# Shared expert of a macaron layer: two groups at once, its down product in the two row halves of the array

## The chip, the cores and the metric

The kernel runs on one core of one Trainium2 chip. The metric is the device time of one execution in microseconds; the median of several runs is compared. All data is float32. Engines: PE is TensorE (matrix products into PSUM), DVE is VectorE, ACT is ScalarE, POOL is GpSimd, SP issues DMAs.

## The reference, cut to what matters

`x` is 8 sequences of 1024 rows of 128. Each goes through an FFN with half weight, attention, and the same FFN again:

```
x = x + 0.5 * ffn(layernorm(x))
x = x + attention(layernorm(x))        # rotary, causal, one head of 128
x = x + 0.5 * ffn(layernorm(x))

ffn(xt):                               # 16 experts of 64 units, top 4 of them
    scores = sigmoid(xt @ gate_w.T);  idx = top_k(scores + gate_b, 4)
    comb   = 2.5 * scores / sum(scores over idx), at idx, else 0
    y      = sum over e of comb[:, e] * ((silu(xt @ g_e.T) * (xt @ u_e.T)) @ w2_e.T)
    return y + (silu(xt @ g_s.T) * (xt @ u_s.T)) @ w2_s.T     # shared expert, 64 units
```

All 16 experts are computed for every row and weighted by `comb`. The last line is the shared expert, the part that the change is about.

## The kernel before, in words

**Groups and periods.** A group is 512 rows (4 tiles of 128) of one sequence in one of the two FFN layers; there are 32. One group is the work of one *period*. The activations are held transposed, `hT` (128 features x 512 rows). Periods 2n and 2n+1 are the two halves of one sequence in one layer.

**A period** has slots U0 to U8 and D0 to D8. Slot U(k+1) follows `up(k)` for k = 0 to 7: two products with `hT`, 128 units of gate into bank 2(k%2)+1 (L276) and of up into bank 2(k%2) (L277), then Silu on ACT (`sg`, L279), gate times up on DVE (`hid`, L281), and times the expert weights `cb` on POOL (`hidT`, L282). Then `down(k)` for k = 0 to 7 accumulates 128 units after 128 units into bank 0, which is `y` (L288).

**The shared expert before.** `up_shared` opens every period: one product with `ws`, whose 128 columns are 64 gate and 64 up units, into bank 5 (L266); Silu of its upper 64 partitions into `ss` (L268); DVE multiplies into rows 64 to 127 of `shared` (L269). Rows 0 to 63 of `shared` and of the weights `wsd` hold zeros. `down(8)` is a full product with them, the ninth that accumulates into `y`; then DVE copies `y` to `yT` (L291). In the next period at U3, `add` turns `yT` back (L296) and adds half of it to `x` (L299).

**Jobs between.** Everything else is put into slots by hand, with `at(period, slot, job)`; `run` issues the jobs of a slot after the product of that slot. The order on each engine is the order in which the program issues; nothing reorders it afterwards. Jobs that matter here:

- normalisation and router of the group that comes next or after next: `norm_a`, `norm_b`, `turn`, `route_a` (four products of 128 rows to 32 columns in the four column tiles of the array, L192), `route_b` (L201), `score` (Exp, L206), `top_a` and `top_b` (DVE, at D8), `top_c` (DVE, at U1 of the next period, ends with `comb`, L238), and `spread` at U3: a turn of `comb` on PE (L247), a copy on ACT (L249), DMAs to DRAM and back as `cb` (L251, L257). For group 1 they all lie in period 0, `score` at D0 to `spread` at D4.
- two or three queries a period (periods 3 to 28), each of 128 rows of attention: `scores` (L368 and DVE L372 to L375), `exp` (L379), `turn` of the probabilities (L395, copies L399 on ACT and L401 on DVE), `attend` (L407), which adds to `x` on DVE (L411) and takes statistics (L144, L145). The first query attends at D7, the second turns at D8 and attends at U2 of the next period. In most odd periods a third takes scores at D4 into banks 4 and 5 and turns at U3 and U4 of the next period.
- `project` of a half sequence to q or k (L335, bank 5 or 4; two ACT copies L339 and L340; DVE L341; POOL L342 and L343), at U3 and U4 of two periods for each sequence.

**Banks.** 0 to 3 rotate for `up`, 0 is `y` as well, 4 and 5 serve the shared expert, projections and scores; 6 and 7 alternate for all small jobs (`other_bank`). Whoever writes a bank waits until its reader is done: the first up product of a period (L277, bank 0) waits for the copy of `y`, and a turn at U3 waits for L411 or an L399 two jobs earlier.

Of the kernel before, what the change touches and what calls it, by code (L numbers as in the profile page):

```python
# [9 lines left out]
F32 = mybir.dt.float32  # L10
AF = mybir.ActivationFunctionType
ALU = mybir.AluOpType
# [3 lines left out]
P = 128  # L16
# [10 lines left out]
def kernel(  # L27
# [14 lines left out]
    nc = tc.nc  # L42
# [3 lines left out]
    I = w_sh_down.shape[0]  # L46
# [3 lines left out]
    W = GT * P  # L50
    EI = E * I
    NP = EI // P
# [3 lines left out]
    const = ctx.enter_context(tc.tile_pool(name="const", bufs=1))  # L56
# [3 lines left out]
    work = ctx.enter_context(tc.tile_pool(name="work", bufs=3))  # L60
    big = ctx.enter_context(tc.tile_pool(name="big", bufs=2))
# [6 lines left out]
    def bank(i, n=1):  # L68
        return psum[:, i * W : (i + n) * W]
# [3 lines left out]
    def other_bank():  # L73
        spare[0] += 1
        return bank(6 + spare[0] % 2)

    def tiles_of(ap):
        return ap.rearrange("p (j q) -> p j q", q=P)
# [34 lines left out]
    ws = const.tile([P, 2 * I], F32, name="ws")  # L113
# [8 lines left out]
    wd = const.tile([P, NP, D], F32, name="wd")  # L122
    nc.sync.dma_start(out=wd, in_=w_down.rearrange("(n p) d -> p n d", p=P))

    wsd = const.tile([P, D], F32, name="wsd")
    nc.gpsimd.memset(wsd[:I, :], 0.0)
    nc.sync.dma_start(out=wsd[I:, :], in_=w_sh_down)
    shared = []
    for n in range(2):
        sh = const.tile([P, W], F32, name=f"shared{n}")  # L130
        nc.gpsimd.memset(sh[:I, :], 0.0)
        shared.append(sh)
    wqkv = const.tile([P, 3, D], F32, name="wqkv")
    cs = const.tile([P, 2, S], F32, name="cs")

# [2 lines left out]
    def stats(key, b, tiles):  # L138

        if key not in mvs:  # L140
            mvs[key] = small.tile([P, NT, 2], F32, tag="mv", name=f"mv_{key}", bufs=16)
        for t in tiles:
            st = small.tile([P, 6], F32, tag="st", name=f"st_{key}_{t}")
            nc.vector.bn_stats(st, xs[b][:, t, :])  # L144
            nc.vector.bn_aggr(mvs[key][:, t, :], st)  # L145
# [26 lines left out]
    class Group:  # L172
        def __init__(self, layer, b, g, n):
            self.layer, self.b, self.g, self.n = layer, b, g, n
            self.nm = f"{layer}_{b}_{g}"
            self.key = f"f{layer}_{b}"
# [82 lines left out]
                        in_=pairs[h, ns, :].unsqueeze(0).broadcast_to([I, NP // 2, W]),  # L259
                    )  # L260

        def up_shared(self):
            self.hidT = big.tile([P, NP, W], F32, tag="hidT", name=f"hidT_{self.nm}")
            self.sh = shared[self.n % 2]
            s_ps = bank(5)
            nc.tensor.matmul(s_ps, ws, self.hT, start=True, stop=True)  # L266
            ss = work.tile([P, W], F32, tag="sg", name=f"ss_{self.nm}")
            nc.scalar.activation(ss[I:, :], s_ps[:I, :], AF.Silu)  # L268
            nc.vector.tensor_tensor(self.sh[I:, :], s_ps[I:, :], ss[I:, :], ALU.mult)  # L269

        def up(self, k):

            nm = f"{self.nm}_{k}"
            units = slice(k * P, (k + 1) * P)
            g_ps, u_ps = bank(2 * (k % 2) + 1), bank(2 * (k % 2))
            nc.tensor.matmul(g_ps, wg[:, units], self.hT, start=True, stop=True)  # L276
            nc.tensor.matmul(u_ps, wu[:, units], self.hT, start=True, stop=True)  # L277
            sg = work.tile([P, W], F32, tag="sg", name=f"sg_{nm}")
            nc.scalar.activation(sg, g_ps, AF.Silu)  # L279
            hid = self.hidT[:, k, :]  # L280
            nc.vector.tensor_tensor(hid, u_ps, sg, ALU.mult)  # L281
            nc.gpsimd.tensor_tensor(hid, hid, self.cb[:, k, :], ALU.mult)  # L282

        def down(self, k):
            if k == 0:
                self.y = bank(0)
            w, h = (wd[:, k, :], self.hidT[:, k, :]) if k < NP else (wsd, self.sh)
            nc.tensor.matmul(self.y, w, h, start=(k == 0), stop=(k == NP))  # L288
            if k == NP:
                self.yT = work.tile([P, W], F32, tag="yT", name=f"yT_{self.nm}", bufs=2)  # L290
                nc.vector.tensor_copy(self.yT, self.y)  # L291

        def add(self):
            yp = tiles_of(other_bank())
            for j in range(GT):
                nc.tensor.transpose(yp[:, j, :], self.yT[:, j * P : (j + 1) * P], ident)  # L296
            tiles = slice(self.g * GT, (self.g + 1) * GT)
            xg = xs[self.b][:, tiles, :]
            nc.vector.scalar_tensor_tensor(xg, yp, 0.5, xg, ALU.mult, ALU.add)  # L299
            if self.layer == 1:  # L300
                nc.sync.dma_start(
                    out=out[self.b].rearrange("(t p) d -> p t d", p=P)[:, tiles, :], in_=xg
                )

# [113 lines left out]
    for b in range(LAG, B):  # L420
        order += [(1, b - LAG), (0, b)]
    order += [(1, b) for b in range(B - LAG, B)]
    groups = [
        Group(layer, b, g, 2 * n + g) for n, (layer, b) in enumerate(order) for g in range(NG)
    ]
# [3 lines left out]
    jobs = {}  # L429

    def at(p, slot, *fs):
        jobs.setdefault((p, slot), []).extend(fs)
# [3 lines left out]
    def when(p, slot):  # L436
        return p * len(slots) + slots.index(slot)
# [28 lines left out]
    for b in range(B):  # L466
        h, st = heads[b], starts[b]
        ready = when(turn_of[0, b, 1] + 1, "U7")
        if b == 0:
            p0, p1 = st - 1, st - 1  # L470
            places = ("U8", "D0", "D2", "D3", "D5", "D6", "D7", "D8")
        else:
            p0, p1 = st - 2, st - 1
            places = ("D0", "D3", "D5", "D8", "U1", "U3", "U4", "U6")
        assert ready < when(p0, places[0])
        at(p0, places[0], h.deviations)
        at(p0, places[1], lambda h=h: h.norm(0))
        at(p0, places[2], lambda h=h: h.norm(1))
        at(p0, places[3], lambda h=h: h.turn(0))
        at(p1, places[4], lambda h=h: h.turn(1))  # L480
        at(p1, places[5], lambda h=h: h.project(0, 0))
        at(p1, places[6], lambda h=h: h.project(1, 0))
        at(p1, places[7], lambda h=h: h.values(0))
        at(st, "U3", lambda h=h: h.project(0, 1))
        at(st, "U4", lambda h=h: h.project(1, 1))
        at(st, "U6", lambda h=h: h.values(1))


    for p, gr in enumerate(groups):
        steps = (  # L490
            gr.norm_a, gr.norm_b, gr.turn, gr.route_a, gr.route_b, gr.score, gr.top_a, gr.top_b,
            gr.top_c, gr.spread,
        )
        if p == 1:
            places = [(0, s) for s in ("U1", "U2", "U5", "U6", "U8", "D0", "D1", "D2", "D3", "D4")]
        else:
            places = [(p - 2, s) for s in ("U5", "D1", "D4", "D5", "D7", "D7", "D8", "D8")]
            places += [(p - 1, "U1"), (p - 1, "U3")]
        if p > 0:
            for f, place in zip(steps, places):  # L500
                at(*place, f)
        if gr.layer == 1:
            for t in range(gr.g * GT, (gr.g + 1) * GT):
                assert done[gr.b, t] < when(p - 2, "U5")

        at(p + 1, "U3", gr.add)
        if gr.layer == 0:
            t = gr.g * GT
            for s in ("U5", "U7"):
                at(p + 1, s, lambda b=gr.b, t=t: stats(f"a{b}", b, (t, t + 1)))  # L510
                t += 2


    for b in range(2, B):
        p = turn_of[0, b, 0]
# [13 lines left out]
    def run(p, slot):  # L529
        for f in jobs.pop((p, slot), []):  # L530
            f()

    gr = groups[0]
# [13 lines left out]
    load_attention()  # L547
    load_x(1, 1)
    for p, gr in enumerate(groups):
        gr.up_shared()  # L550
        run(p, "U0")
        for k in range(NP):
            gr.up(k)
            run(p, f"U{k + 1}")
        for k in range(NP + 1):
            gr.down(k)
            run(p, f"D{k}")
    for p in (NPER, NPER + 1):
        for slot in slots:
# [73 lines left out]
```

## Time and profile before

| | us |
|---|---|
| runs shown: median (lowest to highest of 3) | 1019.27 (1018.79 to 1019.46) |
| profiled execution: own time | 1019.8 |
| profiled execution: span | 1018.0 |
| PE busy | 985.1 (97% of the span) |
| DVE busy | 664.4 (65%) |
| ACT busy | 427.1 (42%) |
| POOL busy | 452.1 (44%) |

The span is from the first to the last instruction on the engines; the execution's own time is 1.8 us longer. The page's mean duration of one instruction is from its start to its modelled end; for PE, where products are pipelined, the distance between the starts of neighbours is shorter than that, and the busy time of a group counts overlaps once. "Idle before" in a row is how long that engine stood idle just ahead of instructions of that row, and "<-" names what ended it.

### The profile page before, as it was taken

The page shows a single profiled execution, that of the slowest core. Times are in us where ns is not written, and L with a number is a line of the kernel's source. Part 1 is how long each engine was busy: PE and PEld are TensorE (multiplying, and loading weights), DVE is VectorE, ACT ScalarE, POOL GpSimd, SP SyncE. Part 2 cuts the span into 40 slices and gives each one's busy share as a digit, 9 for nine tenths or more (in the row PEclk, how much of TensorE's full clock was granted, in tenths as well). Part 3 has the DMA queues.
Part 4 walks back from the last instruction along what each step waited for, and adds up shares of the span by engine and source line. Part 5 has one row for each costly group of instructions (what it writes and reads, how often), then busy time and mean ns, then how long its engine had stood idle before and what let it go on. Part 6 is the DMA issues. An engine that isn't in the chain of part 4 may idle for free.

```text
span 1018.0 us, 11428 instructions
## 1 busy us (share of the span) xinstructions
PE 985.1 (97%) x3552; PEld 511.5 (50%) x3552; DVE 664.4 (65%) x2033; ACT 427.1 (42%) x766; POOL 452.1 (44%) x382
## 2 busy tenths in 40 slices
PE   5799999999999999999999999999999999999998
PEld 2344445554555455545554455555554555455443
DVE  3566877667775767667677665766667756665542
ACT  2243544443544454434444444443444444443321
POOL 1445834365425553345525464334644355323433
PEclk9899999999999999999999999999999999999999
DMA  5384331343214530345213451234412342134440
GB/s 149 99 181 105 84 67 30 72 104 85 46 40 94 116 78 9 82 95 115 59 26 85 95 115 40 45 84 94 95 37 51 82 95 66 43 81 95 95 94 22
DMA packets 56750, 80.23 MB, mean 79 GB/s; under 512 B 3504, under 2 KB 23280, under 8 KB 56560
## 3 DMA queue, kind: packets, MB, share of 16 engines
q1 hardware_dynamic: 55680, 78.36, 34.6%
q10 hardware_dynamic: 1008, 1.13, 0.3%
q8 instruction: 28, 0.46, 0.2%
q14 instruction: 34, 0.28, 0.1%
HBM read 74.24 MB, written 5.24 MB: 78 GB/s over the span
## 4 chain that ended last, share of the span: by engine, by line
PE 85%; DVE 9%; issue 2%; ACT 2%; DMA 1%; POOL 0%; SPq 0%; ACTq 0%; POOLq 0%; DVEq 0%
PE psum L288 24%; PE psum L277 18%; PE psum L276 18%; PE psum L368 6%; PE psum L407 6%; PE psum L395 3%; PE psum L335 3%; PE psum L167 2%; PE psum L266 2%; DVE hidT L281 2%; DVE sel L232 1%; PE psum L349 1%; PE psum L192 1%; PE psum L296 1%; DMA cb<-cd 1%
## 5 line engine op out<-in xcount | busy, mean ns | idle before, releaser
L282 POOL TENSOR_TENSOR hidT<-hidT,cb 128x512 f32<-128x512 f32 x256 | 324.2, 1271 | 536.8 <-DVE hidT L281 489.7
L277 PE MATMUL psum<-hT,wu 128*128 128x512 f32 x512 | 263.2, 596 | 5.1 <-DVE hidT L281 5.1
L276 PE MATMUL psum<-hT,wg 128*128 128x512 f32 x512 | 263.5, 596 | 0.0
L279 ACT ACTIVATE sg<-psum 128x512 f32<-128x512 f32 x256 | 152.7, 597 | 231.8 <-PE psum L276 218.9
L288 PE MATMUL psum<-hidT,wd 128*128 128x512 f32 x512 | 246.5, 599 | 0.0
L281 DVE TENSOR_TENSOR hidT<-psum,sg 128x512 f32<-128x512 f32 x256 | 175.2, 686 | 99.9 <-PE psum L277 97.2
L277 PEld LDWEIGHTS psum<-hT,wu 128*128 128x128 f32 x512 | 97.8, 191 | 129.2 <-issue 103.8
L288 PEld LDWEIGHTS psum<-hidT,wd 128*128 128x128 f32 x512 | 89.9, 190 | 80.7 <-issue 74.4
L276 PEld LDWEIGHTS psum<-hT,wg 128*128 128x128 f32 x512 | 89.2, 192 | 65.4 <-issue 62.8
L407 PEld LDWEIGHTS psum<-v,prT 128*128 128x128 f32 x576 | 74.4, 192 | 30.6 <-issue 26.3
L399 ACT COPY prT<-psum 128x512 f32<-128x512 f32 (+2 forms) x64 | 32.4, 506 | 108.1 <-PE psum L395 107.4
L407 PE MATMUL psum<-v,prT 128*128 128x128 f32 x576 | 74.6, 275 | 0.0
L368 PE MATMUL psum<-k,q 128*128 128x512 f32 (+2 forms) x192 | 72.4, 486 | 0.0
L158 DVE TENSOR_SCALAR xn_f<-x,mv_f,rs_f 128x128 f32<-128x128 f32 x128 | 65.8, 574 | 6.5 <-POOL rs_f L151 6.4
L411 DVE SCALAR_TENSOR_TENSOR x<-psum,rl,x 128x128 f32<-128x128 f32 x64 | 22.1, 346 | 68.3 <-PE psum L407 38.9
L395 PEld LDWEIGHTS psum<-ident,pr 128*128 128x128 f32 x288 | 36.7, 141 | 50.2 <-issue 34.2
L368 PEld LDWEIGHTS psum<-k,q 128*128 128x128 f32 x192 | 36.5, 190 | 45.9 <-issue 45.2
L374 DVE TENSOR_REDUCE top<-psum 128x1 f32<-128x128 f32 (+3 forms) x64 | 48.5, 757 | 2.2
L395 PE MATMUL psum<-ident,pr 128*128 128x128 f32 x288 | 47.4, 274 | 1.9 <-DVE x L299 1.9
L379 ACT ACTIVATE pr<-psum,top 128x128 f32<-128x128 f32 (+3 forms) x64 | 47.7, 746 | 0.3
L372 DVE TENSOR_TENSOR psum<-psum,causal 128x128 f32<-128x128 f32 x64 | 19.0, 297 | 42.4 <-PE psum L368 42.0
L268 ACT ACT_TABLE_LOAD x31 | 39.8, 1283 | 8.9 <-PE psum L266 8.8
(81 smaller groups left out, 988.9 us busy)
## 6 DMA issues: line engine op xcount, KB each, us to landing
cb<-cd SPq DMA_DIRECT2D x128, 512.0 KB, 7.9
x<-in_x SPq DMA_DIRECT2D x16, 256.0 KB, 10.4
out_x<-x SPq DMA_DIRECT2D x16, 256.0 KB, 2.4
cd<-cT SPq DMA_DIRECT2D x32, 32.0 KB, 1.9
cs<-in_rope SPq DMA_DIRECT2D x1, 1024.0 KB, 12.1
wd<-in_w_down SPq DMA_DIRECT2D x1, 512.0 KB, 7.8
wg<-in_w_gate ACTq DMA_DIRECT2D x2, 256.0 KB, 7.2
wu<-in_w_up ACTq DMA_DIRECT2D x2, 256.0 KB, 6.4
```

The source lines that it names most:

```text
L158: nc.vector.tensor_scalar(xn[:, j, :], xs[b][:, t, :], mvs[key][:, t, 0:1], rstd[:, j : j + 1], ALU.subtract, ALU.mult,)
L276: nc.tensor.matmul(g_ps, wg[:, units], self.hT, start=True, stop=True)
L277: nc.tensor.matmul(u_ps, wu[:, units], self.hT, start=True, stop=True)
L279: nc.scalar.activation(sg, g_ps, AF.Silu)
L281: nc.vector.tensor_tensor(hid, u_ps, sg, ALU.mult)
L282: nc.gpsimd.tensor_tensor(hid, hid, self.cb[:, k, :], ALU.mult)
L288: nc.tensor.matmul(self.y, w, h, start=(k == 0), stop=(k == NP))
L368: nc.tensor.matmul(s[:, c:e], h.q[:, i * P : width], h.k[:, c:e], start=True, stop=True)
L374: nc.vector.tensor_reduce(top, s[:, :width], AX.X, ALU.max)
L379: nc.scalar.activation(self.pr[:, : self.width], self.s[:, : self.width], AF.Exp, bias=self.top, scale=SCALE, accum_out=self.h.rl[:, self. ...
L395: nc.tensor.transpose(tp[:, j, :], self.pr[:, (k + j) * P : (k + j + 1) * P], ident)
L407: nc.tensor.matmul(o, self.prT[:, j, :], self.h.v[:, j, :], start=(j == 0), stop=(j == i))
```

## The change

Periods 2n and 2n+1 get one shared expert, the new class `Shared`. Its `up` is two products with `ws`, one for each group, into banks 5 and 4; two Silus; DVE puts the first group's 64 units in rows 0 to 63 of one tile `h`, and the second's in rows 64 to 127. Its `down` is four products of 64 rows by 256 columns: `wsd` now holds the weights twice, in both row halves, and `tile_position=(n * I, 0)` puts group n's product in the upper or lower 64 rows of the array, into bank 5 or 4. ACT copies both results to SBUF (`ys`). `down(k)` ends with k = 7, and `close`, in the place of the ninth product, adds `y` and `ys` into `yT` on DVE.

In even periods `Shared.up` is the first job of U0 and `Shared.down` is at U2; for pair 0 they are at D0 and D3 of period 0, `up` ahead of `score`. `project` moves from U3 and U4 to U4 and U5 (for sequence 0 the first two projections keep their places in period 2).

```diff
     wsd = const.tile([P, D], F32, name="wsd")
-    nc.gpsimd.memset(wsd[:I, :], 0.0)
-    nc.sync.dma_start(out=wsd[I:, :], in_=w_sh_down)
-    shared = []
     for n in range(2):
-        sh = const.tile([P, W], F32, name=f"shared{n}")
-        nc.gpsimd.memset(sh[:I, :], 0.0)
-        shared.append(sh)
+        nc.sync.dma_start(out=wsd[n * I : (n + 1) * I, :], in_=w_sh_down)
...
-        def up_shared(self):
-            self.hidT = big.tile([P, NP, W], F32, tag="hidT", name=f"hidT_{self.nm}")
-            self.sh = shared[self.n % 2]
-            s_ps = bank(5)
-            nc.tensor.matmul(s_ps, ws, self.hT, start=True, stop=True)
-            ss = work.tile([P, W], F32, tag="sg", name=f"ss_{self.nm}")
-            nc.scalar.activation(ss[I:, :], s_ps[:I, :], AF.Silu)
-            nc.vector.tensor_tensor(self.sh[I:, :], s_ps[I:, :], ss[I:, :], ALU.mult)
-
...
         def down(self, k):
             if k == 0:
                 self.y = bank(0)
-            w, h = (wd[:, k, :], self.hidT[:, k, :]) if k < NP else (wsd, self.sh)
-            nc.tensor.matmul(self.y, w, h, start=(k == 0), stop=(k == NP))
-            if k == NP:
-                self.yT = work.tile([P, W], F32, tag="yT", name=f"yT_{self.nm}", bufs=2)
-                nc.vector.tensor_copy(self.yT, self.y)
+            nc.tensor.matmul(
+                self.y, wd[:, k, :], self.hidT[:, k, :], start=(k == 0), stop=(k == NP - 1)
+            )
+
+        def close(self):
+
+            self.yT = work.tile([P, W], F32, tag="yT", name=f"yT_{self.nm}", bufs=2)
+            nc.vector.tensor_tensor(self.yT, self.y, self.ys, ALU.add)
...
+    class Shared:
...
+        def up(self):
+            self.h = work.tile([P, W], F32, tag="sh", name=f"sh_{self.pair[0].nm}", bufs=1)
+            for n, gr in enumerate(self.pair):
+                nc.tensor.matmul(bank(5 - n), ws, gr.hT, start=True, stop=True)
+            for n, gr in enumerate(self.pair):
+                s_ps = bank(5 - n)
+                ss = work.tile([P, W], F32, tag="sg", name=f"ss_{gr.nm}")
+                nc.scalar.activation(ss[I:, :], s_ps[:I, :], AF.Silu)
+                nc.vector.tensor_tensor(
+                    self.h[n * I : (n + 1) * I, :], s_ps[I:, :], ss[I:, :], ALU.mult
+                )
+
+        def down(self):
+            H = W // 2
+            for c in (slice(0, H), slice(H, W)):
+                for n in range(2):
+                    rows = slice(n * I, (n + 1) * I)
+                    nc.tensor.matmul(
+                        bank(5 - n)[:, c], wsd[rows, :], self.h[rows, c], start=True, stop=True,
+                        tile_position=(n * I, 0),
+                    )
+            for n, gr in enumerate(self.pair):
+                gr.ys = work.tile([P, W], F32, tag="ys", name=f"ys_{gr.nm}", bufs=2)
+                nc.scalar.copy(gr.ys, bank(5 - n))
...
-            places = ("D0", "D3", "D5", "D8", "U1", "U3", "U4", "U6")
+            places = ("D0", "D3", "D5", "D8", "U1", "U4", "U5", "U6")
...
-        at(st, "U3", lambda h=h: h.project(0, 1))
-        at(st, "U4", lambda h=h: h.project(1, 1))
+        at(st, "U4", lambda h=h: h.project(0, 1))
+        at(st, "U5", lambda h=h: h.project(1, 1))
...
+        if p % 2 == 0:
+            pair = Shared(groups[p : p + 2])
+            if p == 0:
+                at(0, "D0", pair.up)
+                at(0, "D3", pair.down)
+            else:
+                jobs[p, "U0"] = [pair.up] + jobs.get((p, "U0"), [])
+                at(p, "U2", pair.down)
...
     for p, gr in enumerate(groups):
-        gr.up_shared()
         run(p, "U0")
...
         for k in range(NP + 1):
-            gr.down(k)
+            if k < NP:
+                gr.down(k)
+            else:
+                gr.close()
             run(p, f"D{k}")
```

More of the change, by code (lines that the diff above doesn't have):

```diff
@@ L260, in spread @@
                     )
-        def up_shared(self):
-            self.hidT = big.tile([P, NP, W], F32, tag="hidT", name=f"hidT_{self.nm}")
-            self.sh = shared[self.n % 2]
-            s_ps = bank(5)
-            nc.tensor.matmul(s_ps, ws, self.hT, start=True, stop=True)
-            ss = work.tile([P, W], F32, tag="sg", name=f"ss_{self.nm}")
-            nc.scalar.activation(ss[I:, :], s_ps[:I, :], AF.Silu)
-            nc.vector.tensor_tensor(self.sh[I:, :], s_ps[I:, :], ss[I:, :], ALU.mult)
         def up(self, k):
+            if k == 0:
+                self.hidT = big.tile([P, NP, W], F32, tag="hidT", name=f"hidT_{self.nm}")
             nm = f"{self.nm}_{k}"
@@ L303, in add, with __init__ @@
                 )
+    class Shared:
+        def __init__(self, pair):
+            self.pair = pair
+        def up(self):
[21 more added lines that the diff above has]
+                nc.scalar.copy(gr.ys, bank(5 - n))
     class Heads:
```

## The prediction

> **What bounds the kernel now.** I read the page's busy times and its chain first, then the groups by line, then the timeline of single period ends, where the change acts.
>
> ```profile
> PE 985.1 (97%) x3552; PEld 511.5 (50%) x3552; DVE 664.4 (65%) x2033; ACT 427.1 (42%) x766; POOL 452.1 (44%) x382
> ...
> PE 85%; DVE 9%; issue 2%; ACT 2%; DMA 1%; POOL 0%; SPq 0%; ACTq 0%; POOLq 0%; DVEq 0%
> ```
>
> TensorE is the bound nearly everywhere, and VectorE owns most of the rest of the chain. So PE time taken out is span saved, as long as VectorE does not end later there.
>
> ```profile
> L266 PE MATMUL psum<-hT,ws 128*128 128x512 f32 x64 | 33.6, 608 | 0.0
> L288 PE MATMUL psum<-shared,wsd 128*128 128x512 f32 x64 | 32.8, 593 | 0.0
> L192 PE MATMUL psum<-hT,gw 128*32 128x128 f32 x256 | 13.9, 289 | 0.7 <-ACT hT L168 0.7
> L269 DVE TENSOR_TENSOR shared<-psum,ss 64x512 f32<-64x512 f32 x32 | 22.2, 695 | 9.1 <-ACT ss L268 8.4
> L291 DVE COPY yT<-psum 128x512 f32<-128x512 f32 x32 | 22.1, 691 | 28.9 <-PE psum L288 27.9
> L268 ACT ACT_TABLE_LOAD x31 | 39.8, 1283 | 8.9 <-PE psum L266 8.8
> ```
>
> Each 512-column product leaves two records (64 for 32 calls). In the timeline, starts of such records in a row lie 0.429 us apart: 0.858 us a product, which is the price I use, not the mean duration (records overlap). By the same measure 256 columns take 0.216 us a record (scores, L368).
>
> The end of period 6, and slot U3 of period 7:
>
> ```profile
> 229.97 0.59 PE L288 MATMUL psum<-hidT,wd 128*128 128x512 f32 x1
> 230.40 0.39 PE L407 MATMUL psum<-v,prT 128*128 128x128 f32 x2
> ...
> 230.73 1.02 PE L288 MATMUL psum<-shared,wsd 128*128 128x512 f32 x2
> 230.88 0.35 DVE L411 SCALAR_TENSOR_TENSOR x<-psum,rl,x 128x128 f32<-128x128 f32 x1 [4.66 <-PE psum L407]
> ...
> 231.79 0.69 DVE L291 COPY yT<-psum 128x512 f32<-128x512 f32 x1
> 231.81 1.02 PE L266 MATMUL psum<-hT,ws 128*128 128x512 f32 x2
> ...
> 232.91 1.28 ACT L268 ACT_TABLE_LOAD   x1 [0.53 <-PE psum L266]
> ...
> 233.53 0.59 PE L277 MATMUL psum<-hT,wu 128*128 128x512 f32 x1
> ```
>
> ```profile
> 238.91 0.34 DVE L411 SCALAR_TENSOR_TENSOR x<-psum,rl,x 128x128 f32<-128x128 f32 x1
> ...
> 239.31 0.30 PE L247 MATMUL psum<-ident,comb 128*64 128x128 f32 x1 [0.45 <-DVE x L411]
> ```
>
> Two things to see. The copy of y ends at 232.48, and the first u product, which overwrites y's bank 0, starts at 233.53: 1.05 us to spare. And at U3 PE already waits for VectorE, whose queue holds, between them, top_a, top_b, the shared product, hid 0, top_c, hid 1 and this L411.
>
> **The Trainium skill.** "TensorEngine Tiling (Array Packing)", Tiling Modes: tiles run in parallel, and a change of mode drains the array; Gotcha 1 there asks for different PSUM banks for different row tiles, which the change gives (banks 5 and 4). The trace agrees for column tiles: the next product follows 0.35 us after the four router products below (L192, eight records) began, where eight records of 128 columns in a row take 8 x 0.109 = 0.87; and 0.093 us is lost on entry and on exit (a down product ahead of them takes 0.522 for 0.429, their last record 0.202 for 0.109).
>
> ```profile
> 291.80 0.42 PE L192 MATMUL psum<-hT,gw 128*32 128x128 f32 x8
> 292.15 0.70 PE L288 MATMUL psum<-hidT,wd 128*128 128x512 f32 x1
> ```
>
> "TensorE: Matmul & The Clock Gate", Part 3: four row tiles measured 3.07x. No run here shows row tiles. Its Part 1 says ScalarE and VectorE are strict FIFO; the trace agrees, and this is what makes the waits below.
>
> **The change, part by part.** Period p's last routed down product is "d7". All below is relative to it. A change at a boundary is taken up to U3 of the next period.
>
> 1. Down product: 16 pairs lose 2 x 0.858 = 1.716 us and get four 64-row calls of 256 columns, 8 records. If the two row halves run side by side: 4 x 0.216 + 2 x 0.093 = 1.05 us. If a call's two records keep order ahead of the next tile: 5 x 0.216 + 0.19 = 1.27. If nothing overlaps: 8 x 0.216 + 0.19 = 1.91. I take 1.05, since L192's first records of all four tiles start 7 ns apart.
>
> 2. Up product: same count (32), but two at even periods, none at odd ones. PE between d7 and U3 thus loses 1.716 us into an odd period, and into an even one it gains 1.05.
>
> 3. VectorE: L269 stays at 32 x 0.695, two in even periods, none in odd. L291 becomes an add from PSUM and SBUF; hid (L281) has those operands and takes 0.686, so nothing. ScalarE: 32 ys copies at 0.586 (L168's form) = 18.8 us more. At U2 ys waits for the packed product, with sg 2 behind it: packed start T, ys done T+2.45, sg 2 T+3.05; u 2 ends T+2.97, so hid 2 loses 0.1 at most. ACT has room (42%). Table loads (62 in both programs) don't change; in odd periods sg 0 meets it 0.858 earlier than ss did.
>
> 4. project moves one slot later (U3 to U4, U4 to U5): same work. POOL's two 1.27 us steps behind each move with it; hidT 7 is now ready 3.6 us or more before its down product, which covers it. With L341 out of the way of L299, a 0.54 us wait of L395 at U4 (periods 6, 8, 12, 18, 26) goes; a 0.40 us wait at U3 for ACT's prT copy, hidden by project until now, comes.
>
> 5. One DMA more on SP for wsd (0.5 us at 4 us; SP is then idle until 15.5), three memsets fewer on POOL: nothing.
>
> **What VectorE gives back.** Removing the shared down does not let yT start sooner: L145, which ends the L411 work ahead of it, ends at 231.77 anyway. So into odd periods u 0 comes 1.716 earlier and meets y's bank: period 7 waits 0.7. Then at U3 the chain moves only by the missing L269, 0.70 to 0.74, since top_b ends just when ss did (4.82 and 4.83 after d7). So where PE waits at U3 already, or nearly (into 7, 13, 17, 21, 27), the gain is 0.72 to 0.94, 3.9 together, not 1.716 each. Into 3, where project's L341 is ahead of yT and comb (L238) ends 0.1 before PE needs it, it is nothing. In the other ten L411 ends 0.5 to 1.4 us ahead of PE and VectorE, which waits for ss there, starts hid 0 1.4 to 1.8 sooner, or there is no attention (1, 31) and yT starts 1 us sooner with y: 1.716 less a u 0 wait of 0 to 0.17: about 1.64, 16.4 together. Odd: -20.3.
>
> Into even periods PE pays 1.05, VectorE 0.70 or less. Into 2, 4, 14, 24, 30 a U3 wait of about 0.4 to 0.7 takes part of it (cost 0.66 each); into 10 and 20 a wait of 1.15 does (0.70); into 6, 8, 12, 18, 26 it is 1.05 + 0.40 - 0.54 = 0.91; into 16, 22, 28 1.05. Sum 3.3 + 1.4 + 4.55 + 3.15 = +12.4.
>
> Period 0: its front saves nothing, as PE then waits 4.6 us for group 0's cb and the step behind it. Pair 0 is put ahead of score:
>
> ```profile
> 46.34 0.30 PE L247 MATMUL psum<-ident,comb 128*64 128x128 f32 x1 [2.17 <-DVE comb L238]
> ```
>
> PE waits here for comb. Both silus now go before Exp on ACT (sc starts at 44.4, not 40.86), less 0.65 that L210 loses to POOL now: +2.9. Last, the tail of period 31 has no shared down: -0.86.
>
> Sum: -20.3 + 12.4 + 2.9 - 0.9 = **-5.9 us**. The profiled execution took 1019.8 (span 1018.0); that gives 1013.9. The median of the runs, 1019.27, lies 0.5 lower, so **1013.4**.
>
> **Rivals.** (B) *PE alone decides*: VectorE catches up, for instance because ss no longer holds it. Then 16 x (1.716 - 1.05) = 10.7: 1008.6. For it: VectorE is 65% busy; against: the U3 waits in the page's chain (DVE 9%). (C) *Row tiles don't overlap*: 1.91 instead of 1.05, 16 x 0.864 = 13.8 more, of which 2.3 falls into the U3 waits of even periods: -5.9 + 11.5 = +5.6: 1024.9, slower. The point: above about 1.5 us a packed group the change costs time. For it: no row tile in this trace; against: L192. (D) *VectorE bounds every odd boundary*: all 16 give 0.72 (11.5) and not 20.3: +2.9: 1022.2. For it: the U3 waits of five of them; against: the slack that ten have.
>
> **How the numbers follow.** The case above 0.57, its own range 1010 to 1018 (packed group 1.27 adds 2 to 3 us, period 0 is good to 2, the waits to 3); B 0.18; C 0.13; D 0.12. 1008.5 to 1021.0 leaves out C and half of D. 0.2% is 2.0 us, about what a measurement can tell (the three runs lie within 0.7). Faster: 0.53 + 0.18 = 0.71; same: 0.03 from each of the main case and D; slower: 0.23.
>
> **What would show it.** The four 64-row calls: next product about 1.05 us after the first start; 1.9 makes C true. In odd periods, L277's first product waits 0 to 0.9 us for yT; waits at L247 grow into 7, 13, 17. Into even periods those at L296 shrink from 1.15 to 0.8 and 0.72 to 0.3. ACT busy rises by 19 us, PE's busy falls by some 10. sc of period 0 starts near 44. I am wrong in the steps, even at the right sum, if odd boundaries all gain 1.7, or if PE waits for sh before the packed product (I expect none over 0.1).

## Result and profile after

| | before | after |
|---|---|---|
| median of 5 runs each, us | 1019.27 (1018.61 to 1019.54) | 1027.72 (1027.30 to 1029.80) |
| ratio to before, 95% interval | | 1.0089 [1.0074, 1.0104] |
| profiled execution: own time / span, us | 1019.8 / 1018.0 | 1027.3 / 1025.5 |

The change makes the kernel slower by 0.9%, where 0.6% faster was forecast. Times here and below are of runs whose mean granted clock was 0.99 or more; one run of the first experiment, at 0.658 and 1473.56 us, is left out.

The page of the changed kernel, busy times and chain:

```profile
PE 984.1 (96%) x3616; PEld 511.8 (50%) x3616; DVE 670.4 (65%) x2033; ACT 443.2 (43%) x798; POOL 451.0 (44%) x379
...
PE 86%; DVE 6%; DMA 3%; ACT 2%; issue 1%; POOL 1%; SPq 0%; POOLq 0%; DVEq 0%; ACTq 0%
```

Nothing in these two lines looks like a loss: PE is the bound as before, and VectorE's share of the chain has even fallen. The groups that answer to those shown of before (L305 is the up product, L319 the row-tiled down, L310 the multiplication, L282 the closing add):

```profile
L305 PE MATMUL psum<-hT,ws 128*128 128x512 f32 x64 | 30.1, 593 | 0.0
...
L310 DVE TENSOR_TENSOR sh<-psum,ss 64x512 f32<-64x512 f32 x32 | 22.2, 694 | 4.5 <-ACT ss L309 3.6
...
L282 DVE TENSOR_TENSOR yT<-psum,ys 128x512 f32<-128x512 f32 x32 | 21.2, 664 | 21.8 <-PE psum L275 19.3 <-PE psum L196 2.5
...
L319 PE MATMUL psum<-sh,wsd 64*128 64x256 f32 x128 | 18.1, 402 | 0.0
```

The down products did become cheaper: PE is busy with them for 18.1 us, for 16 pairs, in place of 32.8. The loss stands in another row of the page, that of the turn of the probabilities, of before (L395) first and then of after (L417):

```profile
L395 PE MATMUL psum<-ident,pr 128*128 128x128 f32 x288 | 47.4, 274 | 1.9 <-DVE x L299 1.9
```

```profile
L417 PE MATMUL psum<-ident,pr 128*128 128x128 f32 x288 | 48.1, 278 | 10.3 <-DVE x L433 9.6
```

PE now waits 9.6 us there for VectorE's addition to `x` in `attend` (L433, which was L411). It does so at the ends of periods. The timeline of the changed kernel at the end of period 6, the place shown of before:

```profile
234.25 0.38 PE L429 MATMUL psum<-v,prT 128*128 128x128 f32 x2
...
234.47 0.27 PE L196 MATMUL psum<-ident,lt 128*128 128x128 f32 x1
234.73 0.35 DVE L433 SCALAR_TENSOR_TENSOR x<-psum,rl,x 128x128 f32<-128x128 f32 x1 [4.66 <-PE psum L429]
...
235.13 0.44 PE L417 MATMUL psum<-ident,pr 128*128 128x128 f32 x2 [0.39 <-DVE x L433]
...
235.41 1.02 PE L264 MATMUL psum<-hT,wg 128*128 128x512 f32 x2
...
235.54 0.66 DVE L282 TENSOR_TENSOR yT<-psum,ys 128x512 f32<-128x512 f32 x1
...
236.27 0.68 PE L265 MATMUL psum<-hT,wu 128*128 128x512 f32 x1
```

Two banks that take turns explain the new gap. attend (L429) writes one of banks 6 and 7, route_b (L196) the other, and the D8 turn of the second query (L417) the first again. That bank is still being read by the addition to x (L433, 234.73 to 235.08). PE, which was free at 234.58 (0.11 after L196's start), starts L417 at 235.13: 0.55 us lost. Before, the ninth product stood exactly there. The list of waits, of before first, then of after, shows that the wait was there already (columns: total us, times, longest):

```profile
PEld psum L395 <- DVE x L411: 8.7, 26, 0.4
```

```profile
PEld psum L417 <- DVE x L433: 15.8, 26, 0.7
...
PE psum L417 <- DVE x L433: 9.6, 26, 0.4
```

Before, it was only the weight load (PEld) that waited 26 times for L411, ahead of PE's need and beneath the ninth product; after, the product itself does. Measured from start to start of the records, the 26 gaps between L196 and L417 come to 13.9 us; the profile counts 9.6, since it takes PE as busy to the modelled end of the record ahead. "By starts" below means this measure.

### The profile page after: what moved, and what is told of

Same layout as the page of the kernel before. It is cut to its first block, busy times and chain, and to the rows that moved or that the text cites. A ratio compares the mean times of both kernels' runs of the same rounds, so it can differ in the third digit from the quotient of the medians.

```text
span 1025.5 us, 11576 instructions
## 1 busy us (share of the span) xinstructions
PE 984.1 (96%) x3616; PEld 511.8 (50%) x3616; DVE 670.4 (65%) x2033; ACT 443.2 (43%) x798; POOL 451.0 (44%) x379
## 4 chain that ended last, share of the span: by engine, by line
PE 86%; DVE 6%; DMA 3%; ACT 2%; issue 1%; POOL 1%; SPq 0%; POOLq 0%; DVEq 0%; ACTq 0%
PE psum L275 20%; PE psum L264 19%; PE psum L265 19%; PE psum L390 6%; PE psum L429 6%; PE psum L417 4%; PE psum L305 3%; PE psum L357 3%; DMA cb<-cd 2%; PE psum L162 2%; PE psum L319 2%; PE psum L371 1%; PE psum L187 1%; DVE x L433 1%; DVE sel L227 1%
## 5 line engine op out<-in xcount | busy, mean ns | idle before, releaser
L429 PEld LDWEIGHTS psum<-v,prT 128*128 128x128 f32 x576 | 74.4, 192 | 30.6 <-issue 27.3
L429 PE MATMUL psum<-v,prT 128*128 128x128 f32 x576 | 74.6, 275 | 0.0
L153 DVE TENSOR_SCALAR xn_f<-x,mv_f,rs_f 128x128 f32<-128x128 f32 x128 | 69.5, 603 | 7.4 <-POOL rs_f L146 7.3
L433 DVE SCALAR_TENSOR_TENSOR x<-psum,rl,x 128x128 f32<-128x128 f32 x64 | 22.1, 346 | 67.9 <-PE psum L429 39.2
L417 PEld LDWEIGHTS psum<-ident,pr 128*128 128x128 f32 x288 | 34.8, 141 | 47.2 <-issue 29.6
L417 PE MATMUL psum<-ident,pr 128*128 128x128 f32 x288 | 48.1, 278 | 10.3 <-DVE x L433 9.6
L163 ACT COPY hT<-psum 128x512 f32<-128x512 f32 x32 | 18.8, 586 | 52.2 <-PE psum L162 52.2
```

The costliest lines, as they stand in the source:

```text
L153: nc.vector.tensor_scalar(xn[:, j, :], xs[b][:, t, :], mvs[key][:, t, 0:1], rstd[:, j : j + 1], ALU.subtract, ALU.mult,)
L417: nc.tensor.transpose(tp[:, j, :], self.pr[:, (k + j) * P : (k + j + 1) * P], ident)
L429: nc.tensor.matmul(o, self.prT[:, j, :], self.h.v[:, j, :], start=(j == 0), stop=(j == i))
```

## Experiments

**The bank alone.** The changed kernel, with one operand moved:

```diff
-        def turn(self, half):
+        def turn(self, half, b=None):
...
-            tp = tiles_of(other_bank())
+            tp = other_bank()
+            tp = tiles_of(tp if b is None else bank(b))
...
-            at(*t0, lambda q=q: q.turn(0))
+            at(*t0, lambda q=q, b=2 if n == 1 else None: q.turn(0, b))
```

> The changed kernel, in which only the first turn of the second query (D8) writes bank 2, free since its exp, in place of bank 6 or 7. Theory W (the bank): at D8 PE waits 0.50 to 0.58 us for VectorE's x (L433), which still reads the bank that this turn is to write; the ninth product of before stood between and hid that. Then the wait is gone in all 25 periods that have it (13.3 us), but not all of it is span: into odd periods a wait for y's bank of up to 0.7 comes in its place, and where U3 waits for VectorE anyway nothing is gained. About 8 us: 1019 to 1020. Rival V (VectorE and ScalarE simply have too much to do between D7 and U3, and PE waits for them at one place or another): the waits move to U3, and the time stays within 2 us of 1027.7.

Measured: 1015.25 us (five runs, 1014.41 to 1017.90), ratio 0.9963 [0.9951, 0.9975]: 12.5 us less than the changed kernel, and faster than before. The profile of this kernel is of one further run:

> The changed kernel with the D8 turn in bank 2 once more, for its profile: no wait of the D8 turn; in odd periods L265 waits up to 0.7 us for yT; at U3 the waits at L242 and L287 are longer than in the changed kernel. Time 1014 to 1018.

Measured: 1015.5, span 1013.7. The groups of that run:

```profile
L265 PE MATMUL psum<-hT,wu 128*128 128x512 f32 x512 | 264.0, 597 | 9.3 <-DVE hidT L269 6.1 <-DVE yT L282 3.2
...
L418 PE MATMUL psum<-ident,pr 128*128 128x128 f32 x288 | 46.9, 273 | 0.0
...
L242 PE MATMUL psum<-ident,comb 128*64 128x128 f32 x32 | 9.3, 291 | 10.1 <-DVE comb L233 6.7 <-ACT prT L422 1.7 <-DVE x L434 1.6
```

The turn (L418) waits for nothing any more; part of the wait comes back as 3.2 us for yT. More came off than the 8 us expected: I had priced the returning waits too high. By the traces, 13.1 us come off outside period 0, and period 0 takes 1.2 us more (on that period see below). The waits at U3, which were expected to be longer, came to 10.1 us at L242 (10.5 in the changed kernel) and 1.9 at L287 (1.4). The wait is the bank's, not a shortage of VectorE time, which would have moved it whole.

**The cover alone, without any of the change.** The kernel before without its ninth product:

```diff
-            nc.tensor.matmul(self.y, w, h, start=(k == 0), stop=(k == NP))
+            if k < NP:
+                nc.tensor.matmul(self.y, w, h, start=(k == 0), stop=(k == NP - 1))
             if k == NP:
```

> The kernel before without the ninth down product (the shared expert's result is left out of y; its up product, Silu and multiplication stay). Nothing of the change is in it but the missing product. Theory W: the D8 wait of about 0.55 us appears in the 25 attention periods, as in the changed kernel. Of 32 x 0.858 = 27.5 us, 18 could be span (VectorE sets U3 in 11 periods), and 14 x 0.55 = 7.7 of that is lost to the wait: about 1009. Rival V: no wait at D8; all that VectorE leaves is gained: 1001.

Measured: 1008.39 us, ratio 0.9894 [0.9879, 0.9908].

The same with the turn in bank 2, by the same edit as above:

> The same without the ninth product (shared result left out of y), and the D8 turn in bank 2. Theory W: no wait at D8, about 1001, some 8 us under the run without the bank. Rival V: as the run without the bank, within 1 us.

Measured: 1000.25 us, ratio 0.9811 [0.9798, 0.9824]. The turn's row without the product, and without it but with bank 2:

```profile
L396 PE MATMUL psum<-ident,pr 128*128 128x128 f32 x288 | 48.9, 279 | 11.5 <-DVE x L412 9.6 <-DVE x L300 1.9
```

```profile
L397 PE MATMUL psum<-ident,pr 128*128 128x128 f32 x288 | 47.4, 274 | 1.9 <-DVE x L300 1.9
```

Taking the product out of the old kernel brings the same 9.6 us of waiting for x that the change brings; giving the turn its own bank removes exactly these. The 27.5 us of products (32 x 0.858) are worth 11.5 us with the shared bank and 19.6 with a free one (before took 1019.84 in the same series). Pairs, row tiles and ScalarE's copies are not needed for the loss.

**What packing is worth.** In the changed kernel, two full-height products in place of four row-tiled ones:

```diff
-            H = W // 2
-            for c in (slice(0, H), slice(H, W)):
-                for n in range(2):
...
+            for n in range(2):
+                nc.tensor.matmul(bank(5 - n), wsd, self.h, start=True, stop=True)
```

> The changed kernel with the pair's down as two full-height products of 512 columns (both read all 128 rows of h with wsd doubled, so each result is the sum over both groups and y is not the reference's) in place of four row-tiled ones. If packing is worth what the trace says (1.06 us a pair in place of 1.72) and PE is the bound at U2: 16 x 0.66 = 10.6 us more, less about 1 that falls into waits at U3 of periods 4, 10, 20, 24: 1037. If VectorE sets even periods in general: under 1031.

Measured: 1034.58 us, ratio 1.0144 [1.0131, 1.0158]: 6.9 us above the changed kernel, not 10. Timeline of period 10, U2, of the changed kernel, then of this one:

```profile
338.61 0.38 PE L429 MATMUL psum<-v,prT 128*128 128x128 f32 x2
338.93 1.13 PE L319 MATMUL psum<-sh,wsd 64*128 64x256 f32 x8
339.99 1.12 PE L264 MATMUL psum<-hT,wg 128*128 128x512 f32 x2
340.95 1.02 PE L265 MATMUL psum<-hT,wu 128*128 128x512 f32 x2
```

```profile
340.00 1.88 PE L316 MATMUL psum<-sh,wsd 128*128 128x512 f32 x4
341.72 1.02 PE L264 MATMUL psum<-hT,wg 128*128 128x512 f32 x2
342.58 1.02 PE L265 MATMUL psum<-hT,wu 128*128 128x512 f32 x2
```

Read the starts. Full height: 341.72 - 340.00 = 1.72. Packed: 339.99 - 338.93 = 1.06; but the two records ahead take 0.32 where such two take 0.22, and the product behind takes 0.96 where it takes 0.86. So the group costs 1.26, and the gain is 0.46 a pair, the same in all 15 even periods from 2 on.

**project alone**, in the kernel before (U3, U4 to U4, U5):

> The kernel before, in which only project moves one slot later (U3, U4 to U4, U5). By the prediction's item 4: five waits of 0.54 us at the U4 turn go (2.7 us), five of 0.40 us for ACT's prT copy come at U3 (2.0 us): no change, 1018.5 to 1019.5. If POOL's later steps of project hold a product: over 1021.

Measured: 1019.33 us (13 runs), ratio 0.9998 [0.9989, 1.0006]. By starts, the five gaps at the U4 turn (2.7 us) are gone, and the gaps ahead of L247 at U3 grew from 8 with 3.9 us to 13 with 6.3. That is an even trade, as worked out.

**Towards a faster version.** All but one of these stand on top of the bank-2 kernel, and each keeps the edits ahead of it. First, close() ahead of D7's jobs:

```diff
-            else:
+            if k == NP - 1:
                 gr.close()
             run(p, f"D{k}")
```

> The changed kernel with the D8 turn in bank 2, and close() at the head of D7, ahead of attend, in place of D8. VectorE stands idle some 4 us ahead of L433 at D7, so the 0.69 us add goes into idle time. Theory W: no wait for y's bank in odd periods, and what VectorE ends at U3 comes 0.3 to 0.7 sooner: about 4 us under the run with bank 2 alone (1016.3), so 1012. Rival V: VectorE's sum of work is unchanged, so nothing is gained: 1016.

Measured: 1014.96 us (1011.81 to 1015.77), ratio 0.9953 [0.9939, 0.9967]. This is 0.3 us below the bank-2 kernel, whose own runs spread over 3.5, so the medians decide nothing. The traces do: outside period 0 this execution is 2.4 us shorter than that of the bank-2 kernel, not the 4 expected, and its period 0 is 2.7 us longer. Period 0 varies from execution to execution. Here the granted clock was 0.62 from 28 to 37 us and 0.66 from 49 to 54 us; in the next run, whose period 0 is the same program, it was 0.81 and 1.00, and that period ended 3.7 us earlier. Small differences between these versions are therefore read outside period 0. In the profile with close() first the wait for yT at U0 is down from 3.2 to 0.6 us, but the waits at U3 for x come to 2.6 and 1.0 us in place of 1.6 and 1.1.

Then attend of the second query into bank 4 in odd periods (its body takes the bank as `turn` does):

```diff
-            at(*a, q.attend)
+            at(*a, lambda q=q, b=4 if n == 1 and p % 2 == 0 else None: q.attend(b))
```

> As the run with close() first, and in odd periods the second query's attend at U2 writes bank 4, free there, in place of bank 6 or 7; so add and spread at U3 no longer wait for L433. Theory W: in periods 7, 13, 17, 21, 27 the wait at U3 goes from L433 to comb, which ends 1.04 us sooner: about 2.5 us less than without it: 1009.5. If comb is as late: no change.

Measured: 1008.55 us, ratio 0.9902 [0.9888, 0.9916]. The waits for x at U3 are gone. 6.4 us came off and not 2.5. The gaps at U3 account for 3.6 of it (9.2 to 5.7 by starts), and the traces differ by no more than that outside period 0; the rest is the 3.7 us of period 0, which this edit does not touch.

Both bank changes in the kernel before (attend in bank 4 in every period there, which up_shared leaves free):

> The kernel before (no pairs, nine products) with both bank changes: the D8 turn in bank 2 and the second query's attend in bank 4 in every period. Theory W: the D8 turn had no wait there, so its bank does nothing; the waits of L296 and L247 for L411 at U3 (7.0 us in all by the trace) go, and 0.4 of ACT's prT copy comes at six places: about 1015. If this gains as much as the bank changes did with pairs, pairs were not what needed them.

Measured: 1013.33 us (1015 expected), ratio 0.9945 [0.9933, 0.9958]. So banks help without pairs too, and 4.8 us separate this from the version with pairs; since close() is placed differently as well, this is not the worth of pairs alone.

Last, again on top of the version with pairs, spread's turn in bank 5 (groups 2 to 31):

```diff
             ct = other_bank()[:, :P]
+            if self.n > 1:
+                ct = bank(5)[:, :P]
```

> As the run with close() first and attend in bank 4, and spread at U3 turns comb into bank 5 in place of bank 6 or 7 (groups 2 to 31). L242's wait of 0.40 us for ACT's prT copy, at 14 places by the trace of that run, is a wait for the bank, so it goes, unless comb itself is then late: 4 to 5.5 us less, 1003 to 1004.5. If it is comb that L242 waits for: no change, 1008.5.

Measured: **1005.05 us** (1003.89 to 1006.54), ratio 0.9857 [0.9844, 0.9870], the fastest of those that compute the whole layer: 1.4% under before and 2.2% under the changed kernel. The row of spread's turn without and with that edit:

```profile
L242 PE MATMUL psum<-ident,comb 128*64 128x128 f32 x32 | 9.3, 292 | 9.1 <-DVE comb L233 6.7 <-ACT prT L422 1.9
```

```profile
L244 PE MATMUL psum<-ident,comb 128*64 128x128 f32 x32 | 9.1, 285 | 6.9 <-DVE comb L233 6.7
```

The wait for ACT's copy was the bank's; what remains is comb, nearly all of it in the first 60 us (6.1 of 6.7). By medians 3.5 us came off; outside period 0 the traces differ by 4.5, within the 4 to 5.5 expected, and comb is late in four places there (1.5 us by starts). Period 0 was 2.5 us longer in this profile, with a granted clock of 0.62 and 0.66 in the two stretches named above.

## Why the prediction was wrong, and where it held

The stretch from a period's last down record to the next period's, summed from the traces (us against before):

| stretch | predicted | changed kernel | with bank 2 |
|---|---|---|---|
| into the 16 odd periods | -20.3 | -15.4 | -21.6 |
| into the 15 even periods from 2 | +12.4 | +21.9 | +15.1 |
| period 0 | +2.9 | +1.8 | +3.0 |
| tail of period 31 | -0.9 | -0.8 | -0.8 |
| sum | -5.9 | +7.5 | -4.3 |

What the D8 wait cost is the difference of the last two columns in the first two rows: 13.1 us before rounding, of the 13.4 that lie between forecast and result. The other misses nearly cancel. That the bank-2 kernel comes near -5.9 is in part luck: its odd row is 1.3 us better than forecast and its even row 2.7 worse.

- **The step that failed** is item 1, in what stands behind the removed product. I took its 0.858 us as span saved, asked what its removal does to y's bank, and put the wait of the job that follows it on PE at nothing. Next in PE's queue at D8 is the turn, and its bank is read by L411, which ended 0.36 us before the turn began (231.23 and 231.59). Taking 0.858 away leaves it 0.50 short: in 26 attention periods, 13 us; measured, 13.9 by starts, of which 13.1 was span. L411's start and length stand in the timeline that the prediction prints; the turn's start was among the lines left out just below it.
- Item 1's price of the packed group was the second miss: 1.26, not 1.05. Tiles do run side by side, and row halves overlap as the column tiles do. But some 0.10 us is lost at four places, in the product ahead, the first pair of records, the last pair and the product behind, and the prediction counted two, the product ahead and the last records. The one behind could be read of before: the L288 record that the prediction prints behind the router products takes 0.70 us, where one behind another takes 0.59. 15 x 0.2 = 3.1 us is the bulk of what the even row misses.
- "What VectorE gives back" held in kind. With the bank out of the way, periods 7, 13, 17, 21 and 27 gain 0.97 to 1.20, 5.2 together (3.9 predicted), and most others 1.6. yT's bank does make PE wait in odd periods (3.2 us by the profile; 0.6 in period 7, where 0.7 was forecast), but the waits at L247 into 7, 13 and 17 did not grow: by starts they were 0.61, 0.93 and 0.61, and are 0.64, 0.86 and 0.64. In the changed kernel the wait for yT's bank is nearly absent, because the D8 wait comes first.
- Item 4 (an even trade) held by its own run; for item 5 (nothing) there is none, and no wait of PE itself for SP or POOL is on the list of waits. ScalarE's copies are there (L325, 17.2 us; ACT busy went from 427.1 to 443.2) and cost nothing that shows. PE's busy time fell by 1.0 us, not by some 10: packing saves less, and 4.3 us of the D8 gaps count as busy, which explains most of it but not all.
- Period 0: sc starts at 43.3, and D0 to D7 takes 2.9 us more, as worked out; in the changed kernel 1.1 is won back in its front, where the granted clock between 30 and 36 us is 0.76 and not 0.56.
- Of the rivals, (C) is refuted by the starts of L319, and (B) and (D) by the odd row with bank 2: 21.6, where (B) wants 16 x 1.716 = 27.5 and (D) 11.5. None was the D8 wait: the range missed because a wait was missed, not because a chance was misjudged.

## What to carry to other kernels

A product that is removed was also time for somebody else: list the next few jobs of the same queue and, for each, when its inputs and *its output buffer* come free, against its new start. A wait that shows only at the weight load, as these 26 did, can be such a debt, paid by whatever PE does meanwhile. When two buffers in turn serve many jobs, a spare one elsewhere can be worth more than the work that was removed: here three such operands and the place of one add were worth 22.7 us on top of a change that by itself cost over 8. And where versions differ by a few microseconds, sum the trace by stage: a start that was 2.7 us longer hid a gain of 2.4.

## What the runs showed of the hardware

Row tiles of 64 rows in f32 overlap almost fully once under way: the two records of a pair, one in each half, start 7 ns apart, and after the first pair (0.32 us) the pairs follow at 0.216, the time of one 256-column record alone. Entering and leaving them costs some 0.10 us in each neighbouring product and as much in the first and the last pair: 0.4 us of the 0.86 that full overlap would save. The Trainium skill, "TensorEngine Tiling (Array Packing)", Key Properties, says that a mode switch drains the array. That these losses are the price of this drain is a reading; no run here separates it.
